# A four-layer kernel on one core: the mix over rows of its last layer by TensorE, its mean square from moments, and gathers in two quarters around a spreading

## The chip, the cores and the metric

The kernel runs on one core of one Trainium2 chip. A core has engines that run their own instruction streams side by side: PE (TensorE, matrix products and transposes), DVE (VectorE), ACT (ScalarE), POOL (GpSimd, which here issues the indirect DMAs that gather and scatter rows) and SP (SyncE, which issues the plain DMAs). The metric is the time of one execution in device microseconds, smaller is better. Times are compared as medians over runs.

## The reference

`x` is 4 sequences of 1024 rows of 128 f32 numbers. Four layers follow each other, and each is twice "x = layernorm(x + f(x))": once with a mixing step, once with a feed-forward step.

Layers 0 to 2 have a cumulative sum with gates, a quantised linear map, a state-space recurrence, 16 routed experts, causal attention with 16 heads, and 8 experts with low-rank parts. What the change touches is layer 3:

```python
def _L3_attn_ref(query, ...):            # query: sequence of 4 blocks, see below
    rms = jnp.linalg.norm(query, axis=-1, keepdims=True) * e ** (-0.5)
    x = query / (rms + EPS)
    u = silu(einsum('nbe,fe->nbf', x, u_w) + u_b)
    v = silu(einsum('nbe,fe->nbf', x, v_w) + v_b)
    y = toeplitz_mix(v, pos, zero, neg)  # over axis n, which has length 4
    out = u * y
    return einsum('nbf,ef->nbe', out, o_w) + o_b + query
```

The mix over the rows runs over the axis of length 4, the four sequences: at each of the 1024 positions and in each of the 256 channels, y of sequence i is the sum over the sequences j of a coefficient, which depends on the lag i - j (seven lags, -3 to 3) and on the channel's head, times v of sequence j. So it is a 4x4 Toeplitz matrix for each channel. The reference adds the query inside this function and the layer adds it again, which gives the "2x" in the kernel.

The feed-forward of layer 3 sends every row to 4 of 32 experts and adds a shared expert; the sum of the chosen experts is weighted by normalised scores.

## The kernel before

`x` stays on the chip as 32 tiles of 128 rows by 128 numbers, 128 rows to the partitions. They are grouped in 4 quarters of 8 tiles (`quarter(q)`, L207; 8 tiles are 256 positions of the four sequences). The layers work on parts: layer 3 on part a (quarters 0 and 1, "the first half"), part b (quarter 2) and part c (quarter 3); layer 2's experts on three parts a2, m2, n2 by rows.

An expert layer of a part is a chain of steps. *Route* computes scores and, for each row and choice, its place in a list sorted by experts (the `pos...` tile, written by DVE at L1272). *Spread* (L1307) scatters each tile of x by an indirect DMA for each tile and choice into that list in memory: 64 DMAs for part a of layer 3, 32 each for parts b and c. *Experts* (`small_experts`, from L1663 on) loads the list in groups of 512 rows (`xg`), transposes, multiplies with the weights of the expert that a group belongs to (`gu`), applies silu and the product (L1692, L1693), multiplies again (`yp`) and writes the results to a second list (`l3ya`, `l3yb`, `l3yc`). *Shared* (L1635) is the shared expert, straight from the transposed x; its sum goes to x at L1651. *Collect* (L1350) gathers, again by indirect DMAs (tile `yt`, 4 per tile of x), and adds the weighted rows to x at L1361. *Finish* normalises and writes out. `indirect` (L1295) is the line of every indirect DMA; POOL issues them one after the other in the order written.

`l3_attn` (L1512 on) is layer 3's mixing step of one part, a loop over its quarters. It normalises the quarter (`norm`, L185: moments by `bn_stats` and `bn_aggr`, L191 and L192, a reciprocal root, then one DVE instruction per tile, L205). Then, for two groups of four tiles each: the square (L1548), its sum (L1549), the root, a scale and the reciprocal (`rms`); x times that (`sq`, L1562), and "2x + bias" in place (L1564). It transposes `sq` to `xq`, makes v and u for two halves of the channels by PE (tile `s`) and ACT (L1531), mixes the four blocks of v on DVE (tile `y`; 4 instructions for each of 4 results and 2 halves, L1590 and L1592), multiplies by u (L1594 or L1596), and multiplies by the output weights on PE, which are added to x. Then it normalises once more and transposes into `xT`.

Part a uses `exps=True`: its silu is made from tanh (L1531 to L1536, more work on DVE), its roots by a Newton iteration on DVE (`rsqrt`, L171), so that ACT keeps the function table that the attention of layer 2 beside it needs. Parts b and c use ACT's Silu and Sqrt and change tables.

The order of the work is written by generators. A step yields its estimated cost in microseconds. `mix(main, side, pace)` (L233) takes a step of the main generator, adds its cost to a due time and takes steps of the side generator until theirs, times the pace, have used it up. Instructions of the side go behind those of the main stream on PE, ACT, DVE and POOL. So a yield's cost decides where the side's instructions stand in every engine's queue, but no engine waits for it. `press` takes steps of the side until a condition holds; `when` makes the side wait until one does; `abreast` interleaves generators. In `all`, part a's attention goes beside layer 2's second attention, and part b's beside the experts of part a. The spreading of b and the gathers of a are abreast with attention and routing of c. Behind these come the spreading of c, then the gathers of b. Then `close` gathers part c and writes it out.

Of the kernel before, what the change touches and what calls it, by code (L numbers as in the profile page):

```python
# [20 lines left out]
P = 128  # L21
# [48 lines left out]
def tile_of(b, i):  # L70

    return i // 2 * QT + b * 2 + i % 2


class Kernel:
# [109 lines left out]
    def norm(self, tiles, by="act"):  # L185
# [11 lines left out]
        else:  # L197
            ve = self.tile(self.small, [P, n], f"ve{n}")
            nc.vector.tensor_scalar(ve, mv[:, :, 1], LN_EPS, None, ALU.add)
            if by == "pool":  # L200
                nc.gpsimd.tensor_tensor(rstd, ve, self.mhalf[:, :n], ALU.pow)
            else:
                self.rsqrt(rstd, ve)
        for t, x in enumerate(tiles):
            nc.vector.tensor_scalar(x, x, mv[:, t, 0:1], rstd[:, t : t + 1], ALU.subtract, ALU.mult)  # L205
# [1306 lines left out]
    def l3_attn(self, part, exps=False):  # L1512
# [5 lines left out]
        with ExitStack() as ctx:  # L1518
# [19 lines left out]
            for q in range(part.q0, part.q0 + part.nq):  # L1538
                s = slice(q * QT, (q + 1) * QT)
                self.norm(self.quarter(q), by="dve" if exps else "act")  # L1540
                yield (7.0,)
                xq = self.tile(vp, [P, QC], "xq")
                rms = self.tile(self.small, [P, QT], "rms")
                for g in range(2):
                    sg = slice(q * QT + g * 4, q * QT + g * 4 + 4)
                    r = rms[:, g * 4 : g * 4 + 4]
                    sq = self.tile(vp, [P, 4, D], "sq")
                    nc.vector.tensor_tensor(sq, x[:, sg, :], x[:, sg, :], ALU.mult)  # L1548
                    nc.vector.tensor_reduce(r, sq, AX.X, ALU.add)  # L1549
                    if exps:  # L1550

                        ri = self.tile(self.small, [P, 4], "rmsi")
                        v = self.tile(self.small, [P, 4], "rmsv")
                        nc.vector.tensor_scalar(v, r, 1e-30, None, ALU.max)
                        self.rsqrt(ri, v)
                        nc.vector.tensor_tensor(r, r, ri, ALU.mult)
                    else:
                        nc.scalar.activation(r, r, AF.Sqrt)
                    nc.vector.tensor_scalar(r, r, float(np.float32(D ** -0.5)), 1e-8, ALU.mult, ALU.add)
                    nc.vector.reciprocal(r, r)  # L1560
                    yield (4.0,)
                    nc.vector.tensor_tensor(sq, x[:, sg, :], r.unsqueeze(2).to_broadcast([P, 4, D]), ALU.mult)  # L1562

                    stt(  # L1564
                        x[:, sg, :], x[:, sg, :], 2.0, self.row["l3_ob"].unsqueeze(1).to_broadcast([P, 4, D]),
                        ALU.mult, ALU.add,
# [507 lines left out]
```

## Time and profile before

| | before |
| --- | --- |
| median of 11 runs | 2526.1 us (2519.64 to 2537.42) |
| profiled execution, its own time | 2525.85 us |
| its span in the profile | 2524.1 us |
| granted clock of PE, mean | 0.825 |
| instructions in the span | 28678 |
| PE matmul records, busy | 1707.7 us (68%) |
| DVE busy | 1345.2 us (53%) |
| ACT busy | 828.8 us (33%) |
| POOL busy | 767.4 us (30%) |
| indirect DMA of POOL, gathers to `yt` in layer 1, mean of one | 945 ns |

The stages of the second half, by the first and last instructions of each in the trace (us from the span's start): layer 2's attention with layer 3's part a beside it, 1285 to 1660; experts m2 and the routing of part a, 1667 to 1784; spreading of part a and gathers of m2, 1784 to 1892; experts n2, to 1941; shared expert and gathers of n2, to 1987; experts of part a with attention and routing of b beside them, 1989 to 2101; spreading of b (2105 to 2146) and gathers of a's first 32 (2147 to 2187), with shared b and attention of c beside them; experts b, 2206 to 2339, with gathers of a's second 32 in spaced groups (2228 to 2284) and the spreading of c (2284 to 2325); shared c and gathers of b, to 2401; experts c, to 2470; gathers of c and the end.

How to read it: busy is the time in which an engine worked on an instruction; a busy share of the whole span is an average over stages with different limits. PE and PEld are the same engine's matmuls and weight loads, which overlap. An f32 matmul is two records in the trace, and one with 512 columns takes about 0.86 us at full clock. A granted clock of 0.50 means that PE runs at half speed.

### The profile page before, as it was taken

The numbers are of one execution on the slowest core, as the hardware profiler recorded it, in microseconds if no ns is written. First come the engines' busy times: TensorE is split into PE (matmuls) and PEld (weight loads), VectorE is DVE, ScalarE is ACT, GpSimd is POOL, SyncE is SP. The second block draws the span as 40 slices with busy tenths as digits, with TensorE's granted clock in tenths as the row PEclk, the third lists the DMA queues.
The fourth block names the chain that finished last, engine by engine and source line by source line (L and its number), as shares of the span: only waits on it lengthen the run. The fifth ranks groups of instructions, "written<-read, shape, count | busy, mean of one in ns | idle before, by whom it ended". The sixth has DMA issues, their size and how long they took to land.

```text
span 2524.1 us, 28678 instructions
## 1 busy us (share of the span) xinstructions
PE 1707.7 (68%) x9605; PEld 1037.2 (41%) x9605; DVE 1345.2 (53%) x3801; ACT 828.8 (33%) x1193; POOL 767.4 (30%) x701
## 2 busy tenths in 40 slices
PE   6535776985652864787788878878628896383490
PEld 3224333852321444655433232355415684173280
DVE  8857894655651643334536663654503575263363
ACT  5510461432320431222255545622102353131140
POOL 5521384136044004323220002011470204435404
PEclk9766788997775977998889889988858998586795
DMA  9900002434101032312300000030410231132242
GB/s 307 288 3 0 16 35 94 122 126 162 40 33 42 20 138 92 99 47 68 106 20 13 1 1 18 1 134 30 169 64 19 83 116 64 47 106 70 63 126 60
DMA packets 225735, 192.05 MB, mean 76 GB/s; under 512 B 17008, under 2 KB 204272, under 8 KB 225072
## 3 DMA queue, kind: packets, MB, share of 16 engines
q1 hardware_dynamic: 204880, 147.28, 18.4%
q0 software_dynamic: 20704, 42.86, 5.2%
q8 instruction: 83, 1.36, 0.2%
q14 instruction: 68, 0.56, 0.1%
HBM read 93.47 MB, written 96.60 MB: 75 GB/s over the span
## 4 chain that ended last, share of the span: by engine, by line
PE 37%; DVE 16%; another core or an unknown queue 15%; issue 8%; ACT 3%; DMA 2%; POOL 2%; SPq 0%; DVEq 0%; POOLq 0%; ACTq 0%
PE gu L157 10%; PE s L157 9%; PE sc L157 5%; PE yp L157 5%; PE tp L165 4%; POOL yt L1295 2%; DVE x L205 1%; DVE pr L1057 1%; PE py L157 1%; ACT pr L1051 1%; DVE x L1361 1%; PE pu L157 1%; PE pg L157 1%; DVE bn L191 1%
## 5 line engine op out<-in xcount | busy, mean ns | idle before, releaser
L1051 ACT ACTIVATE pr<-sc 128x1024 f32<-128x1024 f32 x288 | 279.6, 1021 | 325.9 <-PE sc L157 203.8
L157 PE MATMUL gu<-ld,xgT 128*128 x768 | 203.7, 410 | 95.9 <-ACT xgT L167 40.7
L157 PE MATMUL sc<-qm,kT 32*128 32x512 f32 (+3 forms) x1536 | 202.6, 564 | 14.7 <-ACT pr L1051 8.1
L157 PEld LDWEIGHTS gu<-ld,xgT 128*128 128x128 f32 x768 | 147.0, 202 | 125.4 <-issue 51.2
L157 PE MATMUL s<-pr,va 128*32 128x512 f32 (+3 forms) x1536 | 173.6, 527 | 31.9 <-issue 12.8
L157 PE MATMUL gu<-wall,xgT 128*128 x352 | 181.5, 642 | 2.7 <-ACT xgT L167 2.0
L169 DVE COPY hT<-tp 128x512 f32<-128x512 f32 x140 | 96.0, 686 | 150.3 <-remote 71.7
L165 PE MATMUL tp<-ld,hg 128*128 128x128 f32 x736 | 118.8, 284 | 78.2 <-DVE hT L169 41.3
L1693 DVE TENSOR_TENSOR hg<-sg,gu 128x256 f32<-128x256 f32 x192 | 78.7, 417 | 138.6 <-ACT sg L1692 108.2
L165 PEld LDWEIGHTS tp<-ld,hg 128*128 128x128 f32 x736 | 94.7, 147 | 138.2 <-DVE hT L169 47.9
L1057 DVE TENSOR_TENSOR pr<-pr,ld 128x512 f32<-128x512 f32 (+1 forms) x160 | 92.5, 581 | 103.5 <-ACT pr L1051 101.2
L167 ACT COPY xgT<-tp 128x512 f32<-128x512 f32 x118 | 69.1, 586 | 220.1 <-PE tp L165 148.7
L157 PEld LDWEIGHTS sc<-qm,kT 32*128 32x128 f32 x1536 | 86.1, 199 | 120.7 <-issue 75.0
L1692 ACT ACTIVATE sg<-gu 128x256 f32<-128x256 f32 x192 | 72.5, 383 | 185.0 <-PE gu L157 99.7
L1466 ACT ACTIVATE sg<-gu 128x512 f32<-128x512 f32 x88 | 52.4, 597 | 242.7 <-PE gu L157 130.7
L1295 POOL DMA_INDIRECT l1ra<-x,posl1a x64 | 93.6, 1462 | 61.0 <-DVE posl1a L1272 41.8
L165 PE MATMUL tp<-ld,xg 128*128 128x128 f32 x472 | 79.5, 297 | 47.2 <-ACT hT L167 25.2
L157 PE MATMUL yp<-ld,hT 128*128 x768 | 104.2, 278 | 3.7 <-issue 2.1
L1295 POOL DMA_INDIRECT yt<-l1yr,posl1r x64 | 60.5, 945 | 146.4 <-DVE x L1361 80.2
L1468 DVE TENSOR_TENSOR hg<-sg,gu 128x512 f32<-128x512 f32 x88 | 60.0, 682 | 84.0 <-ACT sg L1466 69.9
L157 PE MATMUL yp<-wall,hT 128*128 x704 | 98.6, 286 | 1.5 <-DVE hT L169 1.5
L157 PE MATMUL pu<-xT,ld 128*128 128x512 f32 x104 | 62.5, 696 | 52.7 <-DVE hs L736 32.5
(433 smaller groups left out, 3528.1 us busy)
## 6 DMA issues: line engine op xcount, KB each, us to landing
wall<-wall SPq DMA_DIRECT2D x16, 768.0 KB
l3ra<-zero SPq DMA_DIRECT2D x1, 6144.0 KB
ld<-in_l_w SPq DMA_DIRECT2D x2, 3072.0 KB
wall<-we SPq DMA_DIRECT2D x24, 256.0 KB
ld<-in_l_w SPq DMA_DIRECT2D x1, 6144.0 KB
xg<-l3ra SPq DMA_DIRECT2D x24, 256.0 KB
l3ya<-yg SPq DMA_DIRECT2D x24, 256.0 KB
l1ra<-zero SPq DMA_DIRECT2D x1, 5120.0 KB
```

The lines of the kernel that those rows point to most:

```text
L157: return self.nc.tensor.matmul(out, lhsT, rhs, start=start, stop=stop)
L165: nc.tensor.transpose(pt[:, k * P : (k + 1) * P], s, self.ident)
L167: nc.scalar.copy(dst, pt[:, : n * P])
L169: nc.vector.tensor_copy(dst, pt[:, : n * P])
L191: nc.vector.bn_stats(st, x)
L1051: nc.scalar.activation(pr, sc[h], AF.Exp)
L1057: nc.vector.tensor_tensor(d, d, cst["tril"].unsqueeze(1).unsqueeze(1).to_broadcast([P, 2, n, P]), ALU.mult)
L1295: ins = self.nc.gpsimd.indirect_dma_start(**kw)
L1466: nc.scalar.activation(sg, gu[:, 0, :], AF.Silu)
L1468: nc.vector.tensor_tensor(h, sg, gu[:, 1, :], ALU.mult)
L1692: nc.scalar.activation(sg, pg[:, :, 0, :], AF.Silu)
L1693: nc.vector.tensor_tensor(h[:, 2 * c : 2 * c + 2, :], sg, pg[:, :, 1, :], ALU.mult)
```

## The change

Six things are done.

1. `norm` can apply its mean and scale on ACT (`on_act`): one Identity activation per tile in place of a DVE instruction, and one small DVE instruction for the offset. Parts b and c use it in `l3_attn`, twice per quarter.
2. The mean square that `rms` needs is taken from the variance of the moments, times the squared scale: after normalising, the mean of a row is zero. Squares and their sums go, and the short chain of root, scale and reciprocal is done once for 8 tiles and not twice for 4.
3. The output bias is added by PE, as a product of a row of ones with the bias row that starts each sum, and "2x" moves to the addition of the result.
4. For parts b and c the mix is done by PE: for each lag a diagonal matrix with the lag's coefficients (`mixes`, 14 of 128x128) multiplies the blocks of v that have this lag, and the products are summed in PSUM. 20 matmuls per quarter, with up to 512 columns each, 8192 columns in all; DVE keeps one product with u per two blocks. The diagonals are made by 14 DVE instructions (`l3_mixes`) beside layer 2's experts n2. Part a keeps the mix on DVE.
5. The gathers of part a ("first half") are split: quarter 0 (32 DMAs) stays behind the spreading of b, and quarter 1 (32 DMAs) goes behind the spreading of c. Each half finishes its own quarter.
6. The costs that the steps yield change with it, so the side's steps stand at other places among those of the main stream. The built program of PE grows from 21192 to 21477 instructions.

The branch behind the flag at the end of `all` gets the same calls; it does not run with these inputs.

```diff
-    def norm(self, tiles, by="act"):
+    def norm(self, tiles, by="act", on_act=False):
...
+        if on_act:
+            off = self.tile(self.small, [P, n], f"off{n}")
+            nc.vector.scalar_tensor_tensor(off, mv[:, :, 0], -1.0, rstd, ALU.mult, ALU.mult)
         for t, x in enumerate(tiles):
-            nc.vector.tensor_scalar(x, x, mv[:, t, 0:1], rstd[:, t : t + 1], ALU.subtract, ALU.mult)
+            if on_act:
+                nc.scalar.activation(x, x, AF.Identity, bias=off[:, t : t + 1], scale=rstd[:, t : t + 1])
+            else:
+                nc.vector.tensor_scalar(x, x, mv[:, t, 0:1], rstd[:, t : t + 1], ALU.subtract, ALU.mult)
+        return mv, rstd
...
-                self.norm(self.quarter(q), by="dve" if exps else "act")
+                mv, rstd = self.norm(self.quarter(q), by="dve" if exps else "act", on_act=not exps)
                 yield (7.0,)
                 xq = self.tile(vp, [P, QC], "xq")
                 rms = self.tile(self.small, [P, QT], "rms")
+                if exps:
+                    v = self.tile(self.small, [P, QT], "rmsv")
+                    nc.vector.tensor_scalar(v, mv[:, :, 1], 1e-30, None, ALU.max)
+                    self.rsqrt(rms, v)
+                    nc.vector.tensor_tensor(rms, rms, mv[:, :, 1], ALU.mult)
+                else:
+                    nc.scalar.activation(rms, mv[:, :, 1], AF.Sqrt)
+                nc.vector.tensor_tensor(rms, rms, rstd, ALU.mult)
+                nc.vector.tensor_scalar(rms, rms, 1e-8, None, ALU.add)
+                nc.vector.reciprocal(rms, rms)
+                yield (2.0,)
                 for g in range(2):
...
-                    nc.vector.tensor_tensor(sq, x[:, sg, :], x[:, sg, :], ALU.mult)
-                    nc.vector.tensor_reduce(r, sq, AX.X, ALU.add)
...
-                    yield (4.0,)
                     nc.vector.tensor_tensor(sq, x[:, sg, :], r.unsqueeze(2).to_broadcast([P, 4, D]), ALU.mult)
-                    stt(
-                        x[:, sg, :], x[:, sg, :], 2.0, self.row["l3_ob"].unsqueeze(1).to_broadcast([P, 4, D]),
-                        ALU.mult, ALU.add,
-                    )
...
+                    if not exps:
+                        for i0 in range(0, B, 2):
+                            y = self.tile(ps, [P, 2, TQ], "s")
+                            lags = [0, -1, -2, -3, 1] if i0 == 0 else [0, 1, 2, 3, -1]
+                            for lag in lags:
+                                lo, hi = max(i0, lag), min(i0 + 2, B + lag)
+                                self.mm(
+                                    y[:, lo - i0 : hi - i0, :], self.mixes[:, c * 7 + (lag if lag >= 0 else 3 - lag), :],
+                                    v[:, lo - lag : hi - lag, :], lag == 0, lag == lags[-1],
+                                )
+                            nc.vector.tensor_tensor(u[:, c, i0 : i0 + 2, :], u[:, c, i0 : i0 + 2, :], y, ALU.mult)
+                            yield (4.5,)
+                        continue
...
+                        self.mm(py[:, k, :], self.cst["all1"][0:1, :], self.row["l3_ob"][0:1, :], True, False)
                         for c in range(NC):
-                            self.mm(py[:, k, :], u[:, c, b, h * P : (h + 1) * P], wo[:, c, :], c == 0, c == NC - 1)
+                            self.mm(py[:, k, :], u[:, c, b, h * P : (h + 1) * P], wo[:, c, :], False, c == NC - 1)
                     sg = slice(q * QT + g * 4, q * QT + g * 4 + 4)
-                    nc.vector.tensor_tensor(x[:, sg, :], py, x[:, sg, :], ALU.add)
+                    stt(x[:, sg, :], x[:, sg, :], 2.0, py, ALU.mult, ALU.add)
...
+    def l3_mixes(self, ctx):
+        mp = self.pool(ctx, "l3m", right=True)
+        self.mixes = self.tile(mp, [P, 14, P], "mixes")
+        for k in range(14):
+            self.nc.vector.tensor_scalar(self.mixes[:, k, :], self.ident, self.col["toep"][:, k : k + 1], None, ALU.mult)
+            if k % 4 == 3:
+                yield (1.0,)
...
-    def last(self, part, yp):
-        yield from self.collect("l3", part, K3, yp)
-        yield from self.finish(part)
+    def last(self, part, yp, q=0):
+        yield from self.collect("l3", part, K3, yp, q * QT, QT)
+        yield from self.finish(part.q0 + q)
...
-                    on = self.chain(on, self.rows_in(m2))
+                    on = self.chain(on, self.l3_mixes(c3), self.rows_in(m2))
...
-                        self.chain(self.spread("l3", b, K3), self.when(listed("made l3a")), self.last(a, yp)),
+                        self.chain(self.spread("l3", b, K3), self.when(listed("made l3a")), self.last(a, yp, 0)),
                         self.chain(self.l3_attn(c), self.l3_route(c)),
                     ),
-                    self.spread("l3", c, K3), self.when(listed("made l3b")), self.last(b, yp),
+                    self.spread("l3", c, K3), self.last(a, yp, 1), self.when(listed("made l3b")), self.last(b, yp),
```

## The prediction

> **What bounds the kernel now.** I read the page first, then busy times by stage, then what PE waits for, then PE's timeline in the stage that looked worst. The page: no engine is full, and the chain that ended last is carried by PE most, with DVE second.
>
> ```profile
> PE 1707.7 (68%) x9605; PEld 1037.2 (41%) x9605; DVE 1345.2 (53%) x3801; ACT 828.8 (33%) x1193; POOL 767.4 (30%) x701
> ...
> q8 instruction: 83, 1.36, 0.2%
> ...
> PE 37%; DVE 16%; another core or an unknown queue 15%; issue 8%; ACT 3%; DMA 2%; POOL 2%; SPq 0%; DVEq 0%; POOLq 0%; ACTq 0%
> ```
>
> So a DVE saving counts only where PE waits for DVE. The table by stage (start:end, length, then busy of PE, PEld, DVE, ACT, POOL, granted clock, DMA share, GB/s) shows where that is:
>
> ```profile
> 1335.00:1385.00 50.00, 42.66 (x335) 15.17 (x329) 34.42 (x119) 30.59 (x33) 0.00 (x0) 0.93 0.00 1
> ...
> 1989.00:2101.00 112.00, 106.37 (x664) 92.20 (x665) 83.97 (x254) 60.08 (x112) 0.00 (x0) 0.98 0.37 110
> 2101.00:2147.00 46.00, 21.69 (x69) 11.24 (x69) 20.86 (x72) 12.12 (x16) 31.89 (x33) 0.72 0.16 60
> 2147.00:2187.00 40.00, 7.53 (x8) 1.50 (x6) 3.77 (x9) 3.15 (x5) 30.09 (x32) 0.50 0.18 51
> ...
> 2284.00:2325.00 41.00, 8.60 (x43) 7.30 (x41) 8.87 (x26) 2.70 (x6) 31.39 (x32) 0.63 0.17 65
> ```
>
> First row: layer-2 attention with layer 3's part a on the side; PE has gaps. Second: experts of part a with the mix of part b on the side; PE is full. The last three: POOL issues indirect DMAs back to back, and *all* other engines nearly stop. PE's timeline there (start, duration, instruction, idle before):
>
> ```profile
> 2121.04 1.02 PE L157 MATMUL pg<-xT,ld 128*128 128x512 f32 x2
> 2138.68 2.07 PE L157 MATMUL pu<-xT,ld 128*128 128x512 f32 x2 [16.63 <-issue]
> ...
> 2170.88 2.07 PE L157 MATMUL s<-xq,ld 128*128 128x512 f32 x2 [22.58 <-issue]
> 2176.59 2.08 PE L157 MATMUL s<-xq,ld 128*128 128x512 f32 x2 [3.63 <-issue]
> ```
>
> "issue" means that PE waited for nothing the profile shows, 16.6 and 22.6 us long. Queue q8's single packets in the trace give the pattern. There are 83 of 16 KB, one for each 255 of the 21,192 instructions in PE's built program, so I read q8 as PE's code. One lies at 2119.6, inside the POOL run 2105.3-2186.6, and PE crawls from 2121.8 to 2195.5. The other runs look alike: run 1784-1892, packet 1817.0, gaps of 5 to 17 us until 1901; run 2284-2325, packet 2296.2, gaps of 13.3 and 16.1; run 2343-2383, packet 2355.0, a gap of 36.7. Ahead of the packet PE works at full rate beside POOL; from it on PE nearly stops until the run ends, plus some 5 us. The cause is inferred, the pattern is in every long run. From 2101 to the end at 2517 the time is thus mostly PE's work and POOL's runs one after the other.
>
> **The change, part by part.** Per quarter of parts b and c, the mix leaves DVE:
>
> ```profile
> L1592 DVE SCALAR_TENSOR_TENSOR y<-v,ld,y x96: 433/480/486, 1401.2 to 2210.7; 128x256 f32<-128x256 f32 x96
> L1590 DVE TENSOR_SCALAR y<-v,ld x32: 303/346/354, 1400.2 to 2208.4; 128x256 f32<-128x256 f32 x32
> ...
> L1596 DVE TENSOR_TENSOR u<-u,y x16: 416/418/426, 2033.8 to 2211.4; 128x256 f32<-128x256 f32 x16
> ```
>
> 24 x 0.480 + 8 x 0.346 + 8 x 0.418 = 17.6 us of DVE go; 4 products of 128x512 from PSUM come (0.69 each by the equal product into hg, L1468), 2.8 us. On PE 20 matmuls come, 8192 columns in all. A 512-column f32 matmul is two records 0.43 us apart at full clock, so 16 x 0.86 = 13.8 us; at the 2.07 us records of the stalled stretch it would be 33. The output bias adds 8 one-row matmuls of 128 columns per quarter, 0.22 us each by the spacing of py's, 1.8 us, in all four quarters. PE's total: 2 x 13.8 + 4 x 1.8 = 35 us.
>
> (1) *Part a, beside layer-2 attention (1285-1667).* The moments take away, per quarter, two squares and two sums (4 x 0.69), one of two rsqrt chains (first start 1351.2, last end 1354.4: 3.2) and two bias passes (2 x 0.69): 7.5 us, 15 for both quarters. PE gains 3.6 us of bias matmuls. PE is busy 320 of 382 us here, and its waits are mostly on DVE:
>
> ```profile
> PE s L157 <- DVE v L1536: 9.4, 7, 5.7
> PE s L165 <- DVE o L972: 8.0, 6, 4.5
> PE s L157 <- DVE oc L1080: 6.3, 4, 5.3
> ```
>
> At best all 15 were on the path, 15 - 3.6 = -11; at worst none and the matmuls count, +4. I take **-5**: the waits for v and u (9.4 + 3.2) stand near the removed chain, the others behind attention's own operations.
>
> (2) *Experts a with part b's attention (1989-2101).* PE is full: 106.4 of 112 us, and its longest wait, for the first rows of the experts' list (xg, 5.7 us), stays. Added 13.8 + 1.8 = 15.6 us; at least +9 (the idle 5.6 taken up), at most +16. I take **+14**. The DVE and ACT edits here cost nothing: DVE falls from 84 of 112, and ACT, busy 60 of 112, takes 16 normalising passes (under 0.59 each, the 128x512 copy at L167: under 9.4 us) and loses one Sqrt of two with its two table loads (1.28 each). Without PE as cover, DVE's 18 us would be a gain of up to 18. Positions and spread b start 14 later.
>
> The 14 diagonals (14 x 0.35 = 5 us of DVE) are made beside experts n2, where DVE is busy 15 of 49 us: nothing; 5 at worst. The list of part a is ready 2 us of PE work sooner, so the run of 64 spreads starts before two of the last layer-2 results and the 16 gathers become a run of their own. PE is stopped for about as long: **0**, from -10 to +10. SP issues the shared and expert weights a little sooner and l3_uv and l3_o later; those loads land well ahead of use, and the finishing writes become 4+4+4 instead of 8+4, with nothing behind them: 0.
>
> (3) *From spread b to experts b (before 2105-2206: 101 us).* PE's work ahead of experts b rises from 27.6 to 42.5 us at full clock. But where the code packet falls changes too: counted in PE's order, spread b begins at place 76 of a 256-instruction block before and at 251 after. Packets come when PE is at about place 165 to 241, so some 90 to 165 instructions after the run's start before, and 170 to 250 after. So nearly twice as much of the work fits ahead of the stall. The run is unchanged (64 x 1.26 = 81 us). With the 30 us done before the stall, 11 remain behind the run: start of experts b at run + 92, **-9**. Bounds: all done inside the run, 82, -19; phase of no use and the added work paid, +15.
>
> (4) *From experts b to the end (before 311 us to 2517).* Gathers of part a, 33 to 64, no longer go in spaced groups (2228-2284) but behind spread c: one run of 64, 81 us, instead of 41. POOL's wait for them delays nothing: behind them on POOL stand part b's gathers, which wait for experts b anyway. In PE's order the run starts at place 196: the packet falls just ahead of it or just in it. Ahead: the run starts about 66 us after experts b (before 71, with 45.6 us of PE's work done; now 39.7) and ends at 147. Of PE's 62 us of work left before experts c, 34 (a block) go beside it, 28 behind it and the 5 us of restart: experts c start at 180 or 181 instead of 195 (2206 to 2401), **-14**. Inside: PE stands for nearly all of the 81 us; 62 - 5 done late end 17 later, +3. The likelier is "ahead", narrowly: behind a full queue, as here, packets came at place 165 to 175, in smooth flow at 204 to 241.
>
> Sum: -5 + 14 + 0 - 9 - 14 = -14. The profiled execution took 2525.85 us (span 2524.1 and 1.75 around it), 0.25 under the median of 2526.1: 2525.85 - 14 = **2512**.
>
> The Trainium skill, "Runtime: NRT & Kernel Launch", section "Instruction fetch mechanics", speaks against terms 3 and 4: it says that the sequencer fetches blocks of 256 instructions ahead by itself and that a block's boundary is "mostly hidden". Block size and count agree with q8's 83 packets; the gaps of 17 to 37 us do not. By the page the phase would give nothing, and the sum would keep terms 1 and 2 alone: -5 + 14, 2535.
>
> **Rivals.** *A, slower: PE is the bound and POOL's runs are serial with it.* If the packets of runs B and C come as early as before (within 100 instructions of the run's start), all added PE work is paid: 35 - 5 = +30, **2556**. For it: 106 of 112 us busy in stage 2, clock 0.50 in stalled stretches. Against: the places counted above. *B, the packet of spread c's run falls inside it:* term 4 is +3: **2529**. *C, larger gain:* term 1 is -11, attention c is wholly inside run b (-19): -11 + 14 - 19 - 14 = -30, **2496**. For it: PE works beside POOL ahead of its packet. Against: attention c's own chain through ACT and DVE. *D, the change does not do what it says:* the matmuls and products wait on each other so that DVE's saving and PE's cost cancel, all terms near 0: **2526**.
>
> **Numbers.** Forecast (2512, own range 2501 to 2522) 0.35; C 0.18; B 0.15; A 0.27; D 0.05. A measurement of this kernel tells some 0.2% (5 us) from no change. Faster: 0.35 less 0.02 at its upper edge + 0.18 = 0.51. Same: 0.02 + D 0.05 + a third of B 0.05 = 0.12. Slower: A 0.27 + two thirds of B 0.10 = 0.37. The range goes from below C's centre (2488) to just under A's (2550), leaving out the upper half of A (0.14) and a tail of C (0.05).
>
> **What would show it.** Term 1: layer-2 attention's second half ends about 5 us sooner. Term 2: experts a last some 14 us longer with PE still full. Term 3: the stall in run b starts about 30 us after the run's start instead of 16. Term 4: PE works on after spread c begins, and experts c start about 181 us after experts b. Wrong if PE stops early in those runs, or if experts a don't lengthen.

## The result and the profile after

The changed kernel takes 2589.2 us, median of 8 runs (2582.38 to 2594.62), against 2525.2 for the kernel before: a ratio of **1.0255 [1.0237, 1.0272]**. It is 2.5% slower where 2512 us were forecast, and lies above the range of 2488 to 2550. Its profiled execution has a span of 2588.3 us and a mean granted clock of 0.823 (before: 2524.1 and 0.825).

The page of the changed kernel, the same three lines as before:

```profile
PE 1742.0 (67%) x9749; PEld 1061.1 (41%) x9749; DVE 1298.1 (50%) x3655; ACT 828.1 (32%) x1213; POOL 769.7 (30%) x701
...
q8 instruction: 85, 1.39, 0.2%
...
PE 36%; another core or an unknown queue 16%; DVE 13%; issue 5%; ACT 3%; DMA 3%; POOL 1%; SPq 0%; DVEq 0%; ACTq 0%; POOLq 0%
```

DVE lost 47 us of busy time and PE gained 34, which is the 35 us of the prediction. The time grew by 64. So the amounts of work were right, and where they lie was not. The sequence of list writes shows the stages. Each line is one list's write DMAs: operation and count, shortest, median and longest ns, first and last start in us. First the kernel before, then the changed one:

```profile
L1489 SPq DMA_DIRECT2D l2ym<-yg x6: 360/360/500, 1692.3 to 1775.4; - x6
L1711 SPq DMA_DIRECT2D l3ya<-yg x24: 359/360/446, 2002.6 to 2100.3; - x24
L1711 SPq DMA_DIRECT2D l3yb<-yg x16: 359/359/501, 2222.9 to 2339.1; - x16
L1711 SPq DMA_DIRECT2D l3yc<-yg x16: 359/359/367, 2415.1 to 2465.7; - x16
```

```profile
L1497 SPq DMA_DIRECT2D l2ym<-yg x6: 359/360/500, 1724.3 to 1793.8; - x6
L1733 SPq DMA_DIRECT2D l3ya<-yg x24: 359/360/378, 2020.8 to 2138.0; - x24
L1733 SPq DMA_DIRECT2D l3yb<-yg x16: 359/360/367, 2278.1 to 2414.9; - x16
L1733 SPq DMA_DIRECT2D l3yc<-yg x16: 359/359/502, 2451.1 to 2526.5; - x16
```

Subtract line from line. The end of layer 2's experts m2 is 18 us late (7 of that were there already at 1259 us, ahead of all changed instructions; in the traces here, kernels on the slower sort of chip that are alike up to there varied between 1247 and 1263). The end of experts a is 38 late, so they lost some 20. The first result of experts b is 55 late, another 17. Then the first result of experts c is only 36 late: 19 us came back. And its last is 61 late: 25 went again *within* experts c. The end is 64 late.

The table by stage of the changed kernel (start:end, length, busy of PE, PEld, DVE, ACT, POOL, granted clock, DMA share, GB/s): experts a; spread b; first gathers of a; second gathers of a behind spread c; experts c.

```profile
2005.00:2138.00 133.00, 123.74 (x716) 100.85 (x717) 64.46 (x191) 60.98 (x122) 1.89 (x2) 0.98 0.32 96
2145.00:2185.00 40.00, 18.85 (x50) 8.81 (x50) 8.75 (x26) 10.24 (x20) 30.55 (x32) 0.75 0.16 61
2185.00:2227.00 42.00, 8.55 (x32) 5.56 (x32) 0.69 (x1) 1.37 (x2) 30.74 (x33) 0.58 0.18 52
2348.00:2389.00 41.00, 2.59 (x17) 2.40 (x15) 0.84 (x2) 1.35 (x3) 31.09 (x33) 0.54 0.20 59
2460.00:2527.00 67.00, 44.06 (x266) 39.13 (x264) 33.74 (x99) 20.30 (x41) 30.41 (x32) 0.85 0.39 113
```

Experts a are full on PE, as before, only longer. In the runs of gathers PE nearly stops (8.6 us busy of 42, 2.6 of 41). The last row is new: 32 gathers of part b now run beside experts c. In the kernel before they had ended, at 2382, when the first result of experts c was written, at 2415.

The prediction said that PE stops at a code packet of q8. In the changed kernel's trace there is *no* q8 packet between 2136.5 and 2236.9, and PE stops all the same, from about 2168, in the run 2144.9 to 2225.6. In the run 2308.0 to 2389.2 a packet lies at 2306.3, just ahead of the run (the favourable case, as forecast), the next at 2406.2, and PE stops from 2320. Its timeline there:

```profile
2319.55 0.60 PE L165 MATMUL tp<-ld,xg 128*128 128x128 f32 x4
2319.99 1.06 PE L157 MATMUL yp<-ld,hT 128*128 x8
2344.22 3.78 PE L157 MATMUL gu<-ld,xgT 128*128 x8 [23.18 <-issue]
2347.80 1.06 PE L165 MATMUL tp<-ld,hg 128*128 128x128 f32 x4
```

PE has no record for 23.2 us, and the profile names nothing that it waited for. ACT, which waits for PE's results, shows more:

```profile
2343.59 0.58 ACT L167 COPY xgT<-tp 128x512 f32<-128x512 f32 x1 [12.23 <-remote]
2365.28 0.58 ACT L1729 COPY yg<-yp 128x512 f32<-128x512 f32 x1 [21.11 <-remote]
2376.49 0.38 ACT L1714 ACTIVATE sg<-gu 128x256 f32<-128x256 f32 x1 [10.62 <-remote]
2387.68 0.38 ACT L1714 ACTIVATE sg<-gu 128x256 f32<-128x256 f32 x1 [10.82 <-remote]
2398.21 0.58 ACT L167 COPY xgT<-tp 128x512 f32<-128x512 f32 x1 [10.14 <-remote]
```

The copy of `xgT` ends at 2343.59 + 0.58 = 2344.17, and PE's next product, which reads it, starts at 2344.22. So PE did wait for ACT, and ACT had waited for PE's transposes (`tp`), which are on record 24 us earlier, at 2319.55. "issue" in this view does not mean that PE waited for nothing.

The two `sg` stand 11.2 us behind what precedes them, and for each of them PE has, by the program, four matmul records with four weight loads (768 of each for 192 `sg`). That gives an estimate of 11.2 / 8 = 1.4 us for each, where a matmul of these takes some 0.4 us. So PE is not held by one event. Its results come at one instruction in 1.4 us, close to the 1.26 us at which POOL issues its DMAs. "PE stops" is short for this below. Its own records stand in a burst ahead of the results here (24 matmul records from 2344.2 to 2350.6), so this view does not tell whether PE works slowly or whether what it has done is passed on late.

### The profile page after: what moved, and what is told of

Its sections match the earlier page's. It is cut to its first block, busy times and chain, and to the rows that moved or that the text cites. A ratio compares the mean times of both kernels' runs of the same rounds, so it can differ in the third digit from the quotient of the medians.

```text
span 2588.3 us, 28843 instructions
## 1 busy us (share of the span) xinstructions
PE 1742.0 (67%) x9749; PEld 1061.1 (41%) x9749; DVE 1298.1 (50%) x3655; ACT 828.1 (32%) x1213; POOL 769.7 (30%) x701
## 4 chain that ended last, share of the span: by engine, by line
PE 36%; another core or an unknown queue 16%; DVE 13%; issue 5%; ACT 3%; DMA 3%; POOL 1%; SPq 0%; DVEq 0%; ACTq 0%; POOLq 0%
PE gu L157 9%; PE s L157 9%; PE sc L157 5%; PE yp L157 4%; PE tp L165 4%; PE pg L157 1%; ACT pr L1059 1%; PE py L157 1%; PE pu L157 1%; DVE x L1369 1%; DVE pr L1065 1%; POOL yt L1303 1%; DMA xg<-l2rn 1%; DVE bn L192 1%
## 5 line engine op out<-in xcount | busy, mean ns | idle before, releaser
L157 PE MATMUL gu<-wall,xgT 128*128 x352 | 175.1, 623 | 2.0 <-ACT xgT L167 2.0
L157 PEld LDWEIGHTS s<-pr,va 128*32 128x32 f32 x1536 | 38.2, 113 | 153.6 <-issue 104.0
```

The source lines that it names most:

```text
L157: return self.nc.tensor.matmul(out, lhsT, rhs, start=start, stop=stop)
```

## The experiments

Ratios are against the kernel before on the same chip. The chips are of two sorts. On one (e1, e3, e4, e5) the kernel before takes 2102.6 us, on the four others 2514.6 to 2528.9. All kernels compute the whole reference.

The expectations name three theories. **P** is the prediction's: code packets set when a POOL run stops PE. **S**: PE and any long POOL run exclude each other, so all added PE work is paid, and the longer run that the split makes costs too. **Y**: the bias's one-row matmuls are dearer than priced, the changed yields move instructions to worse places, and the mix's PE time is paid.

### The parts alone

**e1**: the changed kernel, part a's gathers in one piece again.

```diff
-                        self.chain(self.spread("l3", b, K3), self.when(listed("made l3a")), self.last(a, yp, 0)),
+                        self.chain(self.spread("l3", b, K3), self.when(listed("made l3a")), self.last2(a, yp)),
...
-                    self.spread("l3", c, K3), self.last(a, yp, 1), self.when(listed("made l3b")), self.last(b, yp),
+                    self.spread("l3", c, K3), self.when(listed("made l3b")), self.last(b, yp),
```

> The changed kernel with the gathers of part a in one piece again, 64 behind the spreading of b, in the order of the kernel before; all else as changed (about 2589). Theory S (PE and long runs of POOL exclude each other, so that the 32 gathers moved from spaced groups into one solid run behind the spreading of c are paid, some 30 us): about 2560. Theory P (what counts is where PE's code packets fall in a run): no fixed sign, within 15 us of 2589. Theory Y (the loss comes from steps that stand earlier in PE's queue and make it wait for DVE): 2589.

Measured 1.0224 [1.0199, 1.0248] (2149.85 to 2102.62). The loss is there without the split.

**e3**: the kernel before with the mix by TensorE (`l3_mixes`, and the block of 20 matmuls in the change's diff), nothing else.

```diff
+                    if not exps:
+                        for i0 in range(0, B, 2):
...
-                    on = self.chain(on, self.rows_in(m2))
+                    on = self.chain(on, self.l3_mixes(c3), self.rows_in(m2))
```

> The kernel before with the mix of parts b and c on TensorE alone (diagonals, 20 matmuls per quarter), no moments, no ACT normalising, gathers as before. S: the added 27.6 us of PE work are paid in full, and DVE's saving buys nothing: about 2553. P: term 2 is +14 and the rest by phase, about 2515 to 2540. Y: as before, 2525, since no step moves against layer 2's attention.

Measured 1.0063 [1.0042, 1.0083]: the mix is a loss by itself.

**e4**: the changed kernel without mix and split: moments, bias by PE, normalising by ACT.

```diff
-                    if not exps:
-                        for i0 in range(0, B, 2):
...
-                    self.spread("l3", c, K3), self.last(a, yp, 1), self.when(listed("made l3b")), self.last(b, yp),
+                    self.spread("l3", c, K3), self.when(listed("made l3b")), self.last(b, yp),
```

> The kernel before with the moments, the bias on PE and the normalising on ACT, but the mix on DVE and the gathers as before. Y: layer 2's attention ends some 13 us later, as in the changed kernel: about 2538. S: PE has 7 us more work, DVE less: 2520 to 2532. The prediction's term 1: about 2520.

Measured 1.0140 [1.0118, 1.0162]. This is the dear part, and it was forecast as a gain; with e3 it makes up e1's loss (0.6 + 1.4 of 2.2%).

**e5**: the kernel before with the split of the gathers alone.

```diff
-                        self.chain(self.spread("l3", b, K3), self.when(listed("made l3a")), self.last(a, yp)),
+                        self.chain(self.spread("l3", b, K3), self.when(listed("made l3a")), self.last(a, yp, 0)),
...
-                    self.spread("l3", c, K3), self.when(listed("made l3b")), self.last(b, yp),
+                    self.spread("l3", c, K3), self.last(a, yp, 1), self.when(listed("made l3b")), self.last(b, yp),
```

> The kernel before with the second half of part a's gathers moved behind the spreading of c, nothing else. S: 32 gathers leave spaced groups beside experts b and join a solid run of 81 us: 2550 to 2560. P: by phase, within 15 us of 2525. Y: 2525.

Measured 0.9962 [0.9941, 0.9984]: a gain of 0.4%, where S expected a loss.

These four ran on the fast chip, and its traces say why the chip is fast. Spread a in e5's trace, then the same step of the kernel before on another chip:

```profile
1571.00:1660.00 89.00, 89.00 (x455) 58.93 (x455) 39.02 (x62) 26.07 (x46) 62.65 (x65) 0.98 0.42 155
```

```profile
1784.00:1871.00 87.00, 45.42 (x175) 26.94 (x173) 18.89 (x30) 10.92 (x19) 61.38 (x64) 0.71 0.37 144
```

The same 64 spreads take the same time on POOL. PE is busy 89 of 89 us beside them on one chip, and 45 of 87 on the other. Experts a, beside which POOL issues few DMAs or none (7 in e5, none in the kernel before), take 114 us on both, from the first row load to the last write. Here, then, POOL's run does not stop PE, and still e1 loses 2.2% and e4 1.4%. S, as the one cause, fell with this, and Y was left to be told apart.

e4's PE timeline, where the output product of part a is made, shows one cause (start, duration, instruction); under it stands the same product of e5, without the bias:

```profile
1253.77 0.48 PE L157 MATMUL s<-rows,ld 1*128 1x128 f32 x2
1254.18 0.71 PE L157 MATMUL s<-ld,u 128*128 128x128 f32 x4
1254.82 0.48 PE L157 MATMUL s<-rows,ld 1*128 1x128 f32 x2
...
1449.72 0.79 PE L157 MATMUL s<-rows,ld 1*128 1x128 f32 x2
1450.44 1.22 PE L157 MATMUL s<-ld,u 128*128 128x128 f32 x4
1451.59 0.79 PE L157 MATMUL s<-rows,ld 1*128 1x128 f32 x2
```

```profile
1457.57 1.95 PE L157 MATMUL s<-ld,u 128*128 128x128 f32 x16
```

With bias one tile takes 1254.82 - 1253.77 = 1.05 us; without, 16 records (four tiles) take 1.95, 0.49 a tile. The one-row product costs 0.56, not 0.22. The second time the tile takes 1451.59 - 1449.72 = 1.87 us, since the granted clock went to 0.5 at 1448.4 and stayed there for 41 us. (It falls there without one-row products too, but for 20.5 us, in the traces of e7 and g2 below.)

### On the slower chips

**e6**: the changed kernel as it is.

> The changed kernel as it is, beside the kernel before on one chip. Theory Y (the moments part loses by order and by dear bias matmuls, the mix by PE time; all of it also where POOL's runs don't stop PE): if the kernel before takes about 2103 here, this takes 2135 to 2150, the whole-gathers run's 2150 less what the split gained alone (8). Theory S (the loss is the exclusion of PE and POOL's long runs): no loss on a chip where that exclusion is absent, about 2103; 2589 where the kernel before takes 2525.

Measured 1.0229 [1.0197, 1.0261] (2572.98 to 2514.57): much as in the result, and the base for e7, e2 and e9, which ran on the same chip.

**e7**: the bias on DVE again.

```diff
+ stt(
+     x[:, sg, :], x[:, sg, :], 2.0, self.row["l3_ob"].unsqueeze(1).to_broadcast([P, 4, D]),
+     ALU.mult, ALU.add,
+ )
...
- self.mm(py[:, k, :], self.cst["all1"][0:1, :], self.row["l3_ob"][0:1, :], True, False)
...
- stt(x[:, sg, :], x[:, sg, :], 2.0, py, ALU.mult, ALU.add)
+ nc.vector.tensor_tensor(x[:, sg, :], py, x[:, sg, :], ALU.add)
```

> The changed kernel with the output bias added by DVE again (2x + bias ahead of the products, sum after), no one-row matmuls; 2.8 us of DVE per quarter come back. Y: in the trace a tile with its bias took 1.06 to 1.87 us on PE against 0.49 without, so 32 tiles cost 18 to 44 us and not 7: 15 to 25 us less than the changed kernel. The prediction's price (0.22 us each): 2 to 7 us less.

Measured 1.0133 [1.0103, 1.0163] (2546.57): **the 32 one-row products cost 2573.0 - 2546.6 = 26 us**, 0.8 each.

**g2**: the bias by PE, but over all 128 rows.

```diff
- self.mm(py[:, k, :], self.cst["all1"][0:1, :], self.row["l3_ob"][0:1, :], True, False)
+ self.mm(py[:, k, :], self.ident, self.row["l3_ob"], True, False)
```

> The changed kernel with the bias product over 128 rows and not one: the identity times the bias row, which every partition holds; as many matmuls of as many columns. If the one-row matmuls are dear because the array changes between 1 and 128 active rows and its granted clock falls to 0.5 beside them: most of the 26 us that the bias on PE cost comes back, ratio to the kernel before 1.013 to 1.017. If it is the number of matmuls and their place in PE's queue: as the changed kernel, 1.023.

Measured 1.0167 [1.0128, 1.0206], between e6 and e7, though on another chip and with intervals that overlap both. Its PE timeline:

```profile
1652.14 0.39 PE L157 MATMUL s<-rows,ld 128*128 128x128 f32 x2
1652.36 0.61 PE L157 MATMUL s<-ld,u 128*128 128x128 f32 x4
1652.81 0.39 PE L157 MATMUL s<-rows,ld 128*128 128x128 f32 x2
```

A tile takes 0.67 us, so this product costs 0.18 to 0.22, the price that the prediction gave the one-row product. One active row among products of 128 is what costs the other 0.4. The weight loads fit this: in g2 a load starts 0.11 us ahead of its matmul (1652.70 and 1652.81), in e4, at each change between one row and 128, only together with it (1254.18 both).

**e2** and **e9**: the place of the side's instructions. `rms` yields its old cost, 8.0 for 2.0, in the changed kernel (e2) and in e7 (e9).

```diff
-                yield (2.0,)
+                yield (8.0,)
```

> The changed kernel with one number other: the step after rms yields 8.0 and not 2.0, so part a's steps keep their places among layer 2's, and SP issues four loads of layer 2's last list ahead of layer 3's expert weights, as before, not one. Y: 8 to 15 us less than the changed kernel in the same call, since the 10 to 15 us wait of layer 2's last experts for these loads goes. S and P: the same as the changed kernel within 5 us.

> Both together: order kept and bias on DVE; the mix on PE, the moments and the split stay. Y: the two savings add, 23 to 40 us less than the changed kernel, so about 2105 where the kernel before takes 2103. S: as the changed kernel.

Measured e2 1.0243 [1.0214, 1.0272], no better than e6, and e9 1.0178 [1.0148, 1.0209], worse than e7. Two amounts stand against each other in the traces, since the same number also moves the steps of parts b and c. From the first gather of a2 to the last write of m2, the stretch with part a's steps, e2 takes 520 us where e6 takes 532; from the first result of experts b to the end it takes 317 where e6 takes 307 (e9 and e7: 511 for 515, and 317 for 304). So the changed place of part a's steps does cost, and these medians do not show it.

The order had also looked like a cause on the fast chip. There SP loads l3_sw and l3_w (6.9 MB) after the first of six row loads and not after the fourth, and experts n2 wait in e4's trace, though not in e5's:

```profile
PE tp L165 <- DMA xg<-l2rn: 15.0, 2, 9.7
```

(total us, times, longest.) There the stretch from the last write of m2 to the first row load of experts a takes 140 us in e1 and e4, and 127 or 128 in e3 and e5. On the slower chips the changed kernel has the same wait (14.8 us), and yet this stretch takes 211 us with it as without: those experts creep beside spread a anyway. With rests (below), where they creep less, it takes 150 us in the changed kernel (h2) and 140 in the kernel before (g4).

**e12**: e7 with the gathers whole. **e13**: e7 with the mix on DVE too. **e8**: e13 with the yield of 8.0.

> The changed kernel with the bias on DVE and the gathers of part a whole behind the spreading of b. So moments, ACT normalising and the mix on PE stay. To set beside the run with the split (ratio to the kernel before 1.013 on the second chip). Theory S (on a chip where long runs of POOL stop PE, the split moves 32 gathers from spaced groups into a solid run): ratio 1.000 to 1.005 there. On a chip like the first (runs don't stop PE), where the split alone gained 0.4%: 1.010. If the split costs nothing on either: 1.013.

> The changed kernel with the bias on DVE and the mix on DVE: moments, ACT normalising and the split stay. If the mix's PE time is paid where PE is full (theory Y and S alike; alone it cost 0.6% where runs don't stop PE, 15 us): ratio 1.000 to 1.008 against 1.013 with it. If DVE's relief pays for it: 1.013.

> As the run before it, with part a's steps at their old places (the step after rms yields 8.0): the moments' gain on DVE without dear bias matmuls, without the early weight load, and with the split. Y: faster than the kernel before, ratio 0.990 to 0.997 where runs don't stop PE (split 8 us, layer 2's attention 5 to 8 us); 0.995 to 1.008 where they do.

Measured e12 1.0110 [1.0080, 1.0140], e13 1.0056 [1.0035, 1.0077], e8 1.0047 [1.0021, 1.0074]. From e7 (1.0133) to e13 is the **mix by PE: 0.8%, some 19 us**, though on another chip. From e12 to e7 is the split: 0.2%, with intervals that overlap, so not shown.

**g1**: e8 with the normalising on DVE again (`on_act=False`). What is left of the change is moments and split.

```diff
-                self.norm(self.quarter(q), by="dve" if exps else "act", on_act=not exps)
+                self.norm(self.quarter(q), by="dve" if exps else "act", on_act=False)
```

> The run with order, split, moments and the mix on DVE (ratio 1.0047), with the normalising of parts b and c on DVE again. So of the change only the moments and the split are left. If ACT's normalising lengthens the chain of parts b and c: ratio 0.997 to 1.002. If not: 1.005, and the split or the moments cost it.

Measured 1.0015 [0.9988, 1.0043]: no difference from the kernel before, so the net loss lies in what was undone: bias, mix and perhaps ACT's normalising. Against e8 the normalising on ACT would cost 0.3%, but the intervals overlap. This is not to say that moments and split do nothing. In g1's trace the first result of experts b comes 10 us sooner than before (2213 to 2223), and from there to the end it takes 317 us, not 301 (e8 and e13: 317 and 318). A gain ahead and a loss behind cancel. That the gain is the moments' and the loss the split's is likely, but no run on these chips has one of them alone.

### What stops PE in a POOL run

If the length of the run is what stops PE, a rest in it should let PE go. The edit in `indirect` queues two small pow instructions on POOL (1.67 us each) behind every eighth DMA. It also puts the time by which the results are expected 5 us later, which moves the additions that follow the gathers:

```diff
+        self.since = getattr(self, "since", 0) + 1
+        if self.rest_after and self.since % 8 == 0:
+            for _ in range(self.rest_after):
+                rest = self.nc.gpsimd.tensor_tensor(self.idle, self.ones[:, :QT], self.mhalf, ALU.pow)
...
+            self.moved_by += 5.0
```

**e10** is the kernel before with rests from layer 3's part a on (48 such instructions in its trace), **g4** with rests from the spreading of part a on (68). **g3** is g1 with the rests of e10, **h2** the changed kernel with those of g4, and **h1** is g1 with rests from layer 2's first attention on (120). With two instructions in each, these are 24, 34 and 60 rests, twice as many as the expectations count.

> The kernel before with two idle POOL instructions (about 2.7 us each) after every 8 indirect DMAs from the spreading of b to the gathers of b, 12 rests. In the trace of before, groups of 8 with 5 us between them stopped PE only some 5 us each, solid runs nearly throughout. S: on a chip where runs stop PE, 10 to 50 us faster (ratio 0.98 to 0.996); where they don't, slower by part of the 65 us of rest (1.000 to 1.015). If what stops PE does not depend on the length of a run: slower on both.

> The kernel before with rests already in the spreading of part a (64 DMAs), 17 rests in all, not 12. If a rest lets PE run in any long run: a further 5 to 20 us, ratio 0.985 to 0.991. If the spreading of a is on the path: the 5 rests of 4 to 5 us are paid, 0.995 to 1.003.

> The same with two idle POOL instructions after every 8 indirect DMAs in the last part, which gave the kernel before a ratio of 0.9927. If that gain comes from the groups alone, it adds: 0.988 to 0.996. If split and rests get at the same idle time: not below 0.997.

> The changed kernel as it is, with the 17 rests that gave the kernel before 0.965. If the change's loss is PE's own (bias and mix matmuls) and order: it stays, 35 to 60 us, ratio to the kernel before 0.980 to 0.990. If the loss is the long runs' (theory S): it goes, ratio 0.960 to 0.970.

> The best version the runs point to: of the change the moments (bias and normalising on DVE) and the split, the mix on DVE, and rests on POOL after every 8 indirect DMAs from layer 2's first attention on, 30 in all, without the last gathers. If rests free PE in every long run: below the kernel before with 17 rests (0.965), 0.930 to 0.960. If the earlier runs are not on the path: 0.960 to 0.970. If the rests of layer 1's gathers are paid: above 0.970.

Measured e10 0.9927 [0.9902, 0.9953], g4 0.9654 [0.9613, 0.9696], g3 0.9753 [0.9716, 0.9791], h2 0.9714 [0.9691, 0.9738], and h1 **0.9078 [0.9058, 0.9098]**, 2293.9 us to 2524.9. POOL does *more* (985 us busy in h1 against 767), and the kernel is 9% faster. The first 86 us of spread a in g4's trace, to be held against the row 1784 to 1871 above:

```profile
1764.00:1850.00 86.00, 80.54 (x407) 53.19 (x406) 35.36 (x54) 23.37 (x42) 69.88 (x64) 0.97 0.39 145
```

PE is busy 80.5 us, not 45. The spreading itself is longer (104 us from first to last, 86 before), and experts n2 end at 1850, not 1941. The same for layer 1's second spreading, the kernel before and then h1:

```profile
716.00:798.00 82.00, 17.74 (x108) 6.83 (x100) 15.22 (x51) 6.03 (x6) 62.14 (x64) 0.58 0.13 51
```

```profile
712.00:821.00 109.00, 79.05 (x623) 36.44 (x623) 62.64 (x165) 38.87 (x40) 89.61 (x79) 0.89 0.14 54
```

17.7 of 82 us busy before, 79 of 109 with rests. So it is the unbroken length of the run that stops PE. The kernel before shows it without any added instruction: where it gathers a's second 32 in groups with pauses (2228 to 2284), PE is busy 42.6 of 56 us. The half of S that says so stands; P, by which the packets decide, does not.

h1 beats both kernels: moments and split from the change, bias, mix and normalising as before, and rests. With rests, moments and split are worth something: g3 against e10, the same rests, is 0.9753 to 0.9927 (on different chips), and from the first result of experts b to the end it takes 279 us where e10 takes 296. The change's own loss shrinks as well: h2 against g4 is 0.9714 to 0.9654, 0.6%, on different chips, and close to the 0.960 to 0.970 by which the loss would be the long runs'. But PE's added work has not become free. In its trace h2 is 44 us behind g4 at the first result of experts b (2173 to 2129), and wins 24 back from there to the end (275 to 298), where the split acts.

## Why the prediction was wrong

**The reading of the bound** was half right. Long runs of indirect DMAs do stop PE, and the rests, worth more than any other edit here, show what that costs. The reason given, "q8 packets", fell by the two runs above: a run with no packet in it, and one with its packet just ahead, stopped PE all the same. The pattern, said to be "in every long run", had been read from four runs of one trace, and a fifth run of that trace is against it. Layer 1's second spreading runs from 716 to 798; its packets lie at 711.8, just ahead of it, and at 746.8. PE, in the kernel before:

```profile
740.07 1.11 PE L165 MATMUL s<-ld,x 128*128 128x128 f32 x4 [8.29 <-issue]
...
745.68 0.42 PE L157 MATMUL s<-pr,va 128*32 128x128 f32 x1 [0.31 <-issue]
748.48 0.37 PE L157 MATMUL s<-pr,va 128*32 128x128 f32 x1 [2.38 <-issue]
749.18 0.37 PE L157 MATMUL s<-pr,va 128*32 128x128 f32 x1 [0.33 <-issue]
751.98 0.37 PE L157 MATMUL s<-pr,va 128*32 128x128 f32 x1 [2.43 <-issue]
```

The first gap and the first slow records come ahead of the packet at 746.8, not behind it. The other sign was read wrongly too. The gaps of 16.6 and 22.6 us that the prediction shows as "issue" end 0.05 us behind DVE's `hs` (2137.95 to 2138.63) and 0.06 us behind ACT's `xq` (2170.24 to 2170.82), which the products that follow read. The Trainium skill ("Runtime: NRT & Kernel Launch", "Instruction fetch mechanics"), by which the cost of crossing a block's boundary is mostly hidden, spoke against this reason, and the runs agree with it: the stops follow no packet.

Against the forecast the stretches are off by 16 us (term 1), 5 (term 2), 25 (term 3) and 23 (term 4 up to the end: +9, not -14). 7 more were there ahead of the change, and 2 lie between experts a and spread b. Together these are the 78 us from -14 to +64.

**Term 1 (-5 forecast).** From the first gather of a2 to the last write of m2 the changed kernel took 11 us more than the kernel before (535 to 524; e6 532). Two things failed. One is the price of the bias, "8 one-row matmuls of 128 columns per quarter, 0.22 us each": the two quarters of part a have 16, and at 0.56 us they cost 9 us, not 3.6, and more where the clock is at half. The other has no price in the term at all: the place of part a's steps, which the changed yields move. The changed kernel has a wait of PE for DVE that the kernel before does not have:

```profile
PE s L165 <- DVE sq L1568: 10.8, 1, 10.8
```

PE's transposes of `sq` stand in its queue ahead of where DVE has `sq` ready. Where the rms step yields 8.0 (e2, e8, e9, g1) this wait is 1.4 us. The stretch takes 532 with one-row products and wait (e6), 520 without the wait (e2), 515 to 523 without the products (e7, e12, e13), and 511 to 517 with neither (e8, e9, g1). Kernels that are alike there differ by up to 8 us, so each of the two is worth some 13, roughly. With neither, DVE's saving shows: 7 to 13 us less than before, where 8.6 (5 and the 3.6 of the bias) were forecast.

**Term 2 (+14).** The mechanism was right. From the first row load of experts a to the last write it is 114 us before, 133 after, 129 in e7 and 114 in e13: mix +15 (13.8 were forecast), bias +4 (1.8 forecast). PE was full, so all of it was paid.

**Run A (0).** Right: from the last write of m2 to the first row load of experts a, 211 us both times. But "those loads land well ahead of use" does not hold: PE waits 14.8 us for row loads of experts n2 that stand behind the weights, which the stop beside spread a hides (see e2).

**Term 3 (-9).** This is the step that failed by its mechanism. From the start of spread b to the first result of experts b: 118 us before, 133 after, 128 in e7, 116 in e13. The added PE work was paid (bias 5, mix 12), since PE stops with the length of POOL's run and not at a packet. "Nearly twice as much of the work fits ahead of the stall" did not come about: the stall came 23 us after the run's start (16 before, 30 forecast) with 19 of PE's 42.5 us done, and lasted through both the spreads and the gathers. On the fast chip, where POOL's run does not stop PE, the added work makes this stretch only 3 to 5 us longer (64 us in e5, 67 in e1, 69 in e3). Rival A, PE serial with POOL's runs, had this right; its sum of 2556 was still too low, for the most part by the bias (26 us, where 7 were priced).

**Term 4 (-14).** From the first result of experts b to the first of experts c the changed kernel took 173 us, 192 before: -19, in the forecast's direction, but not by its mechanism, so this is luck. The packet did lie just ahead of the run, as counted on, and PE stopped 12 us into the run all the same. What left this stretch are the gathers of part b, and the sum left out where they go. Before, they ran beside shared c, ahead of experts c; now the gathers of a's second half stand there, and those of b move into experts c, which last 75 us from first to last write, not 51. From the first result of experts b to the end e7 takes 304 us and e12, without the split, 297: the split costs about 7 in these traces where 14 were forecast as gain. In the medians the two are not told apart. With the mix on DVE the same stretch takes 317 (g1) where the kernel before takes 301.

Two figures of the sums are off by their own terms: 42.5 - 30 leaves 12.5 us behind the run in term 3, not 11, and "inside" in term 4 gives 147 + (62 - 5) = 204, 9 later than 195 and not 3. Neither changes the sign of a term.

**The edits priced at nothing.** "The DVE and ACT edits here cost nothing" holds to 0.3%: normalising on ACT may cost that much (e8 and g1), within their intervals.

In ratio points against the kernel before, on the slower chips: bias 1.0 (on one chip), mix 0.8 and normalising on ACT about 0.3 (from chip to chip, the last within the intervals), moments with split 0.15, which is none within its interval. On the fast chip moments, bias, normalising on ACT and the new order cost 1.4 together, the mix 0.6, and the split gains 0.4: with POOL's runs not stopping PE, it does what it was meant to.

**What stays open.** Why PE's results come at one instruction in 1.4 us while POOL issues DMAs without a rest, whether PE is slow then or what it has done is passed on late, why one chip of five does not do so, and whether a rest helps by the pause or by the other instruction in it. Rests were not tried on the fast chip. In the runs of layer 3 gaps of 20 to 26 us remain with rests (e10, g4). There e10's trace names an ordinary wait: DVE's addition of the shared expert to x waits 16.8 and 21.2 us for the spread's reads of x (DMA `l3rb<-x,posl3b`; twice 8 us on the fast chip in e5). How much of the stop beside spread b this makes in the kernel before, where the same addition has a wait of 14.1 us without a name, was not tried.

## What to carry to other kernels

Before moving work to TensorE, ask whether it is idle *in that stage*: beside experts a it was full, so the added work made them 19 us longer, and DVE's saving there was worth nothing. Look at what ends a gap before giving it a cause: here the instruction that PE needed ended 0.05 us ahead of PE's next start. Price an instruction among the neighbours that it will have: the one-row product cost 0.56 us among products of 128 rows, and 0.22 by its columns. A changed cost of a step moves other steps, and where they go belongs in the sum. When a transfer is moved, write down for every queue what now stands in the place it moved to, all the way to the end of the program.

## What the runs showed of the hardware

- A matmul with one active row between matmuls of 128 rows costs 0.56 us at full clock, the same product over 128 rows 0.2; beside a series of one-row products in e4 the granted clock was 0.5 for 41 us, and for 20.5 us at the same place without them (e7, g2).
- On four of the five chips, after some 10 to 35 us of an unbroken run of 32 to 64 indirect DMAs, PE's results come at about one instruction in 1.4 us. Two small POOL instructions after every eighth DMA give most of PE's rate back: 80.5 of 86 us busy against 45 of 87. With moments and split, which without rests made no difference together, that was 9.2% of the kernel.
- The same kernel takes 2103 us on one chip and 2515 to 2529 on the others. PE's busy share beside POOL is the difference seen (89 of 89 us); experts a, with few of POOL's DMAs or none beside them, take 114 us on both sorts. What a part is worth can differ between the two sorts: the split gains 0.4% on the one, and no gain was seen on the others.
